# Cross-attention block: one unit kind for all attention units, queries kept in SBUF, one-piece subtractions, another order

## The chip, the core and the metric

The kernel runs on one core of a Trainium2 chip. The metric is the time of one execution on the device in microseconds (us); the runs before the change have a median of 717.12 us (714.55 to 719.68 in 3 runs). The engines are TensorE (PE in the profile, PEld for its weight loads), VectorE (DVE), ScalarE (ACT), GpSimd (POOL) and SyncE (SP), which here issues every DMA.

## The reference

Eight sequences of 256 tokens and 512 channels, with a context of the same shape, go through a transformer block with cross-attention and an MLP, all in float32:

```python
x = layer_norm(hidden_states, ln1_w, ln1_b)
q = (x @ q_w + q_b)                      # 16 heads of 32 channels
k = (encoder_hidden_states @ k_w + k_b)
v = (encoder_hidden_states @ v_w + v_b)
scores = einsum('bhqd,bhkd->bhqk', q, k) / sqrt(32)
scores = where(mask, scores, finfo.min)
attn = softmax(scores, axis=-1)
out = einsum('bhqk,bhkd->bhqd', attn, v) @ cproj_w + cproj_b
hidden = out + hidden_states
y = gelu(layer_norm(hidden, ln2_w, ln2_b) @ fc_w + fc_b)   # 2048 wide, tanh form
return hidden + y @ proj_w + proj_b
```

## The kernel before

**Stages.** The sequences are taken in two groups `g` of four (1,024 tokens). For each group the kernel loads context and tokens, normalizes the tokens, transposes both through TensorE (`turn_*`), and makes keys, values and queries (`keys_of` L946, `values_of` L962), then attention (`attention` L1403), the output projection (`output` L1414), the first MLP product (`fc`) and the second (`proj`). Every dense product is done in blocks by a scheme with seven products in place of eight (at two levels in the MLP): sums and differences of the operand blocks (`sums` L834, `minus` and `plus` L645) are made on VectorE or GpSimd, and results are added up on VectorE as they leave the three PSUM banks X, Y and W (`quad` L855). All TensorE work is float32, but for one bf16 product below.

**Units of attention.** A unit `u` = (g, hg, b) is one group `hg` of four heads (4 x 32 = 128 partitions) of one sequence `b`: 256 queries by 256 keys, four heads at once in tiled matmuls. There are 32 units. `units_of` (L1368) gives their order, and in `attention` the scores of unit n stand beside the value products of unit n − 3 (`LOOK = 3`). Queries, keys and values of each unit are loaded from DRAM (`qu`, `ku`, `vu`, 128 KB each; `operands_of` L977), to which `keys_of` and `values_of` stored them in pieces of 256 KB (`qd`, `kd`, `vd`).

There are two kinds of units. `KINDS` sets which is which: the first eight of group 0 are of kind `a`, the other 24 of kind `p`.

- Kind `p` (`scores` L994, `attend` L1037): one score product `s` with the keys on the partitions; ACT copies it out with the mask's bias (`ev`, 8 copies of 128x256, through `copy` L643); VectorE takes the maxima over the keys, by two transposing reductions over 128x1024 (`mx`, L1007), a transpose (`mt`, L1011), three small ACT copies (`mc`, L1014) and a reduction (`fold`, L1015). The 32x32 maxima are stored to DRAM (`md`) and loaded back as a broadcast to all partitions (`mm`, 128x1024, 512 KB). The maxima are subtracted in two halves `less` (L1027), each of them two instructions of 128x512, on VectorE or GpSimd; ACT takes the exponential in place (128x1024, L1030). `attend` makes sums by a product with ones and the value products in one PSUM bank (`av`), VectorE makes the reciprocals (`r`: L1053, L1055, L1056) and multiplies (`att`).
- Kind `a` (`scores_a` L1060, `attend_a` L1116): a first score product `s` with the queries on the partitions; VectorE negates, adds the mask (`mb`) and reduces in one instruction for each head and 128 queries (`max`, L1076, 8 of 128x256, each with an instruction that reads the accumulator); the maxima are split into two bf16 halves (`hl`, L1090 to L1092), transposed (`t2`), stored (`me`) and loaded as rows (`mr`); ACT takes a first exponential only for its row sums (L1082). The reciprocals (`rs`, `tr`, `rd`) go through DRAM and come back in four broadcast loads (`rl`, 32 KB each). A second product `sT` starts from a bf16 product that puts the negated maxima into PSUM, adds the scores with the keys on the partitions, and ACT takes the exponential straight from there (`pt`, L1128). Then value products `av` and `att`.

**The order.** The kernel's code only records operations. `PROGRAM` (L126) is a written-out list of all 3,076 operations in the order in which they are issued; each engine takes its own in that order, and a letter after an operation's name names its engine where there is a choice (`:V` VectorE, `:A` ACT, `:G` GpSimd). `PLACES` (L369) gives each tile its slot in SBUF or its bank in PSUM; a tile waits until the one before it in its slot is done with. `SLOTS` has the number of slots: 44 places of 128x1024 (kind Q; kind P takes halves of them), 14 of 128x256 for `qu`, `ku`, `vu` and `r`. So nothing is decided at run time, and where a wait ends late, all that stands behind it in that engine's list is late. All DMAs are in SP's list, which is in order too.

In the profile L663 is the matmul helper, L654 the addition helper, L630, L635 and L643 copies out of PSUM, L617 and L623 the issue of a load and of a store.

Of the kernel before, what the change touches and what calls it, by code (L numbers as in the profile page):

```python
# [10 lines left out]
F32 = mybir.dt.float32  # L11
U8 = mybir.dt.uint8
BF16 = mybir.dt.bfloat16
# [6 lines left out]
FLT_MAX = 3.4028234663852886e38  # L20
# [3 lines left out]
SLOTS = {"Q": (44, 1024), "P": (36, 512), "H": (14, 256), "sm": (10, 32), "mx": (3, 352), "st": (6, 32), "MB": (4, 256), "MU": (4, 64), "t2": (3, 32), "MR": (3, 256)}  # L24
# [102 lines left out]
cq0_10_1 cq0_01_1 cq0_01_0 cq0_00_1 cq0_00_0 cq0_10_0 vw00 rows6 cq0_11_1 turn_c0_01 xt0_1 turn_c0_11 rows3 c0_01:V  # L127
cq0_11_0 turn_c0_10 rows5 turn_c0_00 kw10 c0_10:V c0_00:A turn_c0_30 c0_11:V kw00 turn_c0_20 xt0_3 c0_30:V c0t1:G
v0_0_P1 mk xt0_2 stats_x0_01 kw11 c0_20:V vw01 turn_c0_21 v0_0_t1:A v0_1_P1 rows2 c0_21:V xt0_0 aggr_x0_01 xt0_6
kws3:V turn_c0_31 rows7 stats_x0_11 k0_0_P1 rows1 c0_31:A stats_x0_10 rows4 aggr_x0_10 xt0_5 kws1:V aggr_x0_11  # L130
rows0 kws2:V v0_0_P2 kw01 eps_x0_1 pow_x0_1 stats_x0_00 xt0_7 vw10 aggr_x0_00 mk~1 c0t3:V v0_1_P2 qw00 fw1_01_0
nb_x0_1 eps_x0_0 v0_0_c11 norm_x0_11:A vw11 pow_x0_0 cols fw1_00_1 k0_0_P7 norm_x0_10:A nb_x0_0 cols~1 pw0_10_10
norm_x0_01:V norm_x0_00:A qw01 c0t2:V v0_1_t1:A xt0_4 turn_x0_00 k0_0_t1:A fw1_00_0 turn_x0_20 c0t4:V k0_0_P6 mu0
x0_20:A stats_x0_21 fw1_11_1 x0_00:A stats_x0_30 fw1_01_1 turn_x0_30 aggr_x0_21 k0_0_t2:V pw0_00_10 turn_x0_10
x0_30:A v0_1_c11 pw0_01_01 k0_0_P5 fw1_10_1 vws1:V pw0_00_11 kws4:V pw0_10_00 k0_0_P2 stats_x0_20 vws2:G mu2
aggr_x0_20 k0_0_t3:V vd0_0_11 fw1i1_3:G pw0_00_00 v0_0_P6 fw1i1_1:V x0_10:V fw1i1_2:G qw10 stats_x0_31 k0_0_P3
eps_x0_2 aggr_x0_30 k0_0_c22 pow_x0_2 k0_0_c11 fw1i2_1:G kd0_0_22 aggr_x0_31 fw1_10_0 eps_x0_3 nb_x0_2 k0_0_P4
pow_x0_3 norm_x0_21:A vu000 fw1i2_3:G nb_x0_3 norm_x0_30:A pw0_10_11 norm_x0_31:V fw0_00_0 qws3:G fw1_11_0
pw0_01_00 norm_x0_20:V turn_x0_11 k0_0_c12:V turn_x0_31 k0_0_c21 turn_x0_21 v0_0_t2:V turn_x0_01 kd0_0_21 x0_21:A
vws3:V v0_0_P5 pw0_11_10 x0_01:A fw1i1_4:V fw1s3:V x0_31:A fcd1_1_True qw11 v0_0_P7 v0_0_t3:A pw0_11_00 fw1i2_2:V  # L140
x0_11:A fw0_10_0 kd0_0_11 q0_1_P2 v0_0_c22 pb fw0_10_1 fw1s1:V kd0_0_12 q0_1_P1 qws1:V fcd1_5_False fw1s2:V
fw0_00_1 q0_0_P1 q0_1_t1:A qws2:V fcd1_6_False x0t1:V q0_0_P2 q0_0_t1:A x0t2:V mb2:V fw1s4:V q0_0_P6 q0_1_c11
x0t3:V q0_1_P6 qd0_1_11 q0_0_t2:A fcd1_3_False vd0_0_22 x0t4:V fcd1_7_False q0_0_P5 pw0_11_11 q0_0_c11 pw0_10_01
fw1i6_3:V fw0_11_1 fw1i2_4:V v0_0_P4 q0_1_t2:V fw1i4_3:G vd0_1_11 qd0_0_11 fw0s3:V fw0_11_0 q0_1_P7 pw0_11_01
fw1i6_1:V cb fw1i5_1:V fw1i6_2:G qu010 ku002 qws4:V q0_1_P5 fcd1_2_True mb0:G v0_0_c21 fw1i4_1:V fw1i5_2:V qu000
q0_0_P7 fw1i5_3:V fw1i5_4:G fw0s1:V k0_1_P1 q0_0_t3:A fw1i6_4:V q0_1_t3:A q0_0_c22 fcd1_6_True q0_0_P3 qd0_0_22
k0_1_t1:A fw0i1_1:V ku020 fw0s2:V pw0_01_10 ku000 fw0i1_2:G q0_0_P4 fcd1_5_True fw1i4_2:V ku022 q0_1_c22 fw0i5_1:G
fw0i5_2:G q0_1_P4 q0_0_c21 fw0i1_4:G q0_0_c12:V qd0_0_21 qd0_1_22 k0_1_P6 q0_1_c21 pw0_00_01 fw0_01_0 fw0i6_3:V
fw1i4_4:V qd0_0_12 vws4:V s000 qu020 fw0i5_4:V fw0_01_1 fw0i6_1:V fw1i3_1:V v0_0_P3 fcd0_5_False max000_5 fw1i3_2:V
fw0i6_2:V max000_2 fw1i3_4:G max000_4 v0_1_P6 fw1i3_3:G v0_0_c12:V fw0i6_4:V vd0_0_12 max000_7 fcd0_6_True max000_6  # L150
q0_1_P3 max000_3 fcd1_3_True fw0i1_3:V qu022 max000_1 max000_0 qu002 fw0i2_1:V s020 fcd1_4_True hl000 ct1_4 fw0s4:V
exp000_7 k0_1_P7 v0_1_t2:A k0_1_t2:A max020_1 fw0i2_2:V q0_1_c12:A max020_0 fw0i2_4:G max020_5 exp000_0 k0_1_P5
t2000 max020_7 fw0i2_3:G exp000_2 max020_2 exp000_1 max020_4 fcd0_2_True max020_3 qd0_1_21 max020_6 s002 k0_1_t3:A
hl020 me000 exp000_5 fcd0_1_True k0_1_c22 k0_1_P2 exp000_4 t2020 max002_0 exp020_5 me020 max002_1 exp000_3
fcd0_6_False max002_3 exp000_6 vd0_0_21 pw0s1:G v0_1_P5 exp020_0 ct1_3 rs000 max002_7 exp020_6 qd0_1_12 max002_4
exp020_2 qu032 max002_5 tr000 k0_1_P4 max002_2 mr000 v0_1_t3:A max002_6 fw0i5_3:G k0_1_c11 hl002 kd0_1_11 s022
# [206 lines left out]
pr17_P4 z1i4_4:G pr14_P6 pr17_c21 pr17_21~1:V out1_1022:G pr14_P2 out1_1012:V pr13_c21 out1_1112:G pr14_t2  # L363
pr17_22~1:V out1_0122:G pr14_P5 out1_0112:G pr17_12:G pr14_P7 out1_0121:G pr14_t3 st1_111 st1_011 out1_1111:V
out1_0111:V pr17_11:V st1_010 pr14_P3 pr17_12~1:V pr17_21:V pr14_c11 st1_110 pr14_c22 pr14_P4 pr14_c12 st1_101
pr14_c21 st1_100
"""

PLACES = """  # L369
# [1150 lines left out]
```

## Time and profile before

| | |
|---|---|
| median of 3 runs | 717.12 us (714.55 to 719.68) |
| profiled execution | 713.26 us |
| its span, first to last instruction | 711.4 us |
| mean granted TensorE clock | 0.999 |
| first score product, first one of kind `p`, last value product | 70.9, 173.7, 410.8 us |
| instructions in the span | 13,452 |

The profile is one execution. Its page gives the busy time of each engine and the costliest groups of instructions: line, engine, operation, tile written and tile read, shape, count, then busy time and mean time of one, then the idle time of the engine just before them and what ended it. TensorE matmuls of float32 show as two instructions each. The trace can be asked for the busy time in any stretch, for all instructions or for those of one tile or line alone, and for the instructions of one engine in order of time.

### The profile page before, as it was taken

How to read it: one execution, taken by the hardware profiler on the slowest of the kernel's cores; microseconds unless marked ns; L12 is line 12 of the kernel's file. 1: busy time of each engine (PE TensorE's matmuls, PEld its weight loads, DVE VectorE, ACT ScalarE, POOL GpSimd, SP SyncE). 2: the span in 40 equal slices, each digit the busy share in tenths (PEclk: the TensorE clock that was granted, in tenths of full speed). 3: DMA queues.
4: the chain of work that ended last, by engine and by line, in shares of the span. 5: the costliest groups of instructions: out<-in, count | busy, mean ns of one | idle time of the engine just before them, and what ended most of it. 6: DMA issues, size and time to landing. Idle time of an engine off the chain costs nothing. (4 is left out here: it accounts for less than half of the span.)

```text
span 711.4 us, 13452 instructions
## 1 busy us (share of the span) xinstructions
PE 682.7 (96%) x4813; PEld 528.5 (74%) x4813; DVE 602.5 (85%) x1125; ACT 345.3 (49%) x775; POOL 325.9 (46%) x310
## 2 busy tenths in 40 slices
PE   8989989999999998999999999999999999999997
PEld 7554555655544575667766789999998888899997
DVE  5988898859999989999899889796888777898863
ACT  1431479968995748967999846001400005730000
POOL 2403352604754567787686655703353004722134
PEclk9999999999999999999999999999999999999999
DMA  8989988888867898768445545338958632851552
GB/s 282 303 289 327 341 265 273 296 282 270 279 211 221 264 300 267 218 196 270 129 155 177 150 130 174 119 104 266 296 163 262 210 100 49 270 164 60 178 193 89
DMA packets 119321, 152.82 MB, mean 215 GB/s; under 512 B 13164, under 2 KB 80344, under 8 KB 119256
## 3 DMA queue, kind: packets, MB, share of 16 engines
q1 hardware_dynamic: 119256, 151.98, 66.7%
q8 instruction: 38, 0.62, 0.3%
q14 instruction: 27, 0.22, 0.1%
HBM read 107.60 MB, written 44.34 MB: 214 GB/s over the span
## 5 line engine op out<-in xcount | busy, mean ns | idle before, releaser
L1027 POOL TENSOR_TENSOR pr<-pr,mm 128x512 f32<-128x512 f32 x64 | 83.9, 1341 | 61.5 <-DMA mm<-md 29.2
L643 ACT ACTIVATE pr<-s,cols 128x256 f32<-128x256 f32 x192 | 77.7, 481 | 9.7 <-PE s L663 5.9
L1285 ACT ACTIVATE h<-h,cols 128x256 f32<-128x256 f32 x128 | 53.9, 496 | 48.8 <-DVE h L654 45.7
L654 DVE TENSOR_TENSOR h<-fc_X,h 128x512 f32<-128x512 f32 x80 | 53.2, 678 | 10.9 <-PE fc_X L663 8.4
L1007 DVE TRANSPOSE_TENSOR_REDUCE mx<-pr 128x32 f32<-128x1024 f32 x48 | 58.0, 1221 | 4.9 <-ACT pr L643 4.9
L1030 ACT ACTIVATE pr<-pr 128x1024 f32<-128x1024 f32 x48 | 50.4, 1061 | 14.2 <-POOL pr L1027 9.6
L1082 ACT ACTIVATE pr<-pr,st 128x256 f32<-128x256 f32 x64 | 32.0, 516 | 17.4 <-DVE st L1092 16.8
L654 DVE TENSOR_TENSOR h<-fc_W,h 128x512 f32<-128x512 f32 x48 | 32.1, 677 | 7.9 <-PE fc_W L663 7.8
L663 PE MATMUL s<-qu,ku 32*128 32x256 f32 x384 | 28.6, 400 | 3.6 <-ACT pt L1128 1.4
L1128 ACT ACTIVATE pt<-sT,cols 128x256 f32<-128x256 f32 x64 | 25.5, 483 | 8.1 <-PE sT L663 4.1
L663 PEld LDWEIGHTS s<-qu,ku 32*128 32x128 f32 x384 | 18.4, 184 | 14.8 <-ACT pr L643 5.5
L630 ACT COPY e<-pr_X 128x256 f32<-128x256 f32 x3 | 1.1, 372 | 57.9 <-PE pr_X L663 57.9
L663 PE MATMUL av<-pr,ones 128*32 128x256 f32 x384 | 26.0, 385 | 1.5 <-ACT pr L1030 0.8
L1027 DVE TENSOR_TENSOR pr<-pr,mm 128x512 f32<-128x512 f32 x32 | 25.9, 857 | 1.8 <-DMA mm<-md 1.8
L654 POOL TENSOR_TENSOR h<-h,fl 128x512 f32<-128x512 f32 x3 | 4.7, 1595 | 48.1 <-DVE fl L654 48.1
L654 DVE TENSOR_TENSOR po<-pr_X,po 128x256 f32<-128x256 f32 x40 | 16.4, 414 | 11.2 <-PE pr_X L663 10.9
L663 PE MATMUL av<-pr,vu 128*32 128x256 f32 x384 | 25.5, 379 | 0.0
L1076 DVE CUSTOM_DVE_ANT_0 pr<-s,mb 128x256 f32<-128x256 f32 x64 | 23.3, 417 | 1.8 <-PE s L663 1.6
L1014 ACT COPY mx<-mx 32x64 f32<-32x64 f32 x72 | 17.5, 243 | 12.7 <-DVE mx L1011 11.2
L663 PE MATMUL fc_W<-y1i,fl 128*128 128x256 f32 x92 | 23.5, 381 | 0.0
L663 PEld LDWEIGHTS av<-pr,ones 128*32 128x32 f32 x384 | 10.5, 109 | 15.0 <-issue 4.9
L630 ACT COPY h<-fc_X 128x512 f32<-128x512 f32 x11 | 6.2, 582 | 31.6 <-PE fc_X L663 31.6
(568 smaller groups left out, 1974.7 us busy)
## 6 DMA issues: line engine op xcount, KB each, us to landing
mm<-md SPq DMA_DIRECT2D x24, 512.0 KB
fl<-fcd SPq DMA_DIRECT2D x48, 256.0 KB
pl<-prd SPq DMA_DIRECT2D x46, 256.0 KB
fl<-prd SPq DMA_DIRECT2D x21, 256.0 KB
fw<-in_L_xattn_fc_w_dram SPq DMA_DIRECT2D x16, 256.0 KB
pw<-in_L_xattn_proj_w_dram SPq DMA_DIRECT2D x32, 128.0 KB
vu<-vd SPq DMA_DIRECT2D x32, 128.0 KB
qu<-qd SPq DMA_DIRECT2D x32, 128.0 KB
```

Of the source, the lines that this page charges most:

```text
L630: (nc.scalar.copy if e == "ACT" else nc.vector.tensor_copy)(to(), of_())
L643: lambda e: nc.scalar.activation(to(), of_(), AF.Identity, bias=bias(), scale=1.0))
L654: E[e].tensor_tensor(to(), in0(), in1(), op)
L663: nc.tensor.matmul(o(), l(), r(), start=first, stop=True, skip_group_check=True)
L1007: T.op(f"mx{u}_{h}", [("DVE", 1.126)], [(pr[h], None)], [(mx, [h])], lambda e, h=h: nc.vector.tensor_reduce(tile_of(mx)[:, 0:64].rearrange ...
L1014: lambda e, a=a: nc.scalar.copy(tile_of(mx)[0:32, 64 + 64 * a : 128 + 64 * a], tile_of(mx)[32 * a : 32 * a + 32, 64:128]))
L1027: E[e].tensor_tensor(p_, p_, at(M, j)[:, None, :].to_broadcast([P, 2, S]), ALU.subtract)
L1030: lambda e, h=h: nc.scalar.activation(tile_of(pr[h]), tile_of(pr[h]), AF.Exp), table="exp")
L1076: nc.vector.tensor_tensor_reduce(at(p_, pk), at(sb[j], i), tile_of(mb), scale=-1.0, scalar=FLT_MAX, op0=ALU.add, op1=ALU.min, accum_out=ti ...
L1082: nc.scalar.activation(at(p_, pk), at(p_, pk), AF.Exp, bias=tile_of(st)[:, 24 + c : 25 + c], scale=-1.0, accum_out=tile_of(st)[:, 16 + c : ...
L1128: nc.scalar.activation(at(pt[j // 2], 2 * (j % 2) + kc), at(sT[j], kc), AF.Exp, bias=col(2 * (4 * g + b) + kc), scale=1.0)
L1285: lambda e, f=f, b=b, c=c: nc.scalar.activation(at(h[f][b], c), at(h[f][b], c), AF.Gelu_apprx_tanh, bias=col(c_fcb + f * 4 + c), scale=1.0 ...
```

## The change

- `KINDS` is `p` for all 32 units. `scores_a` and `attend_a` go, with the tiles, constants, mask tiles and small DMAs that only they use.
- `DIRECT` names the query pieces that need not pass through DRAM. "K": the unit reads its queries in the tile that the projection wrote, and nothing is stored (all eight pieces of group 1). "H": the same for the first half of the piece's columns; the piece is stored and the second half is loaded as before (all eight of group 0). So 8 of 16 query stores and 8 of 32 query loads are left. Keys and values go as before.
- `less` on VectorE is one instruction of 128x1024 for a half; on GpSimd it stays two of 128x512. Of 64 halves the new order gives 28 to VectorE and 36 to GpSimd; before it was 16 and 32 of 48.
- `PROGRAM` and `PLACES` are new throughout: 2,928 operations, with another order and other slots and, for operations that several engines can do, in part another engine. `SLOTS` has 45 places of kind Q for 44. In the built programs GpSimd has 180 additions or subtractions of 512 elements for 151, and 115 of 256 for 109; VectorE has fewer. DMA issues are 577 for 651.

```diff
-SLOTS = {"Q": (44, 1024), "P": (36, 512), "H": (14, 256), "sm": (10, 32), "mx": (3, 352), "st": (6, 32), "MB": (4, 256), "MU": (4, 64), "t2": (3, 32), "MR": (3, 256)}
+SLOTS = {"Q": (45, 1024), "P": (36, 512), "H": (14, 256), "sm": (10, 32), "mx": (3, 352)}
...
-KINDS = ("aaaaaaaapppppppp", "pppppppppppppppp")
+DIRECT = {
+    "q0_0_11": "H", "q0_0_12": "H", "q0_0_21": "H", "q0_0_22": "H", "q0_1_11": "H", "q0_1_12": "H",
+    "q0_1_21": "H", "q0_1_22": "H", "q1_0_11": "K", "q1_0_12": "K", "q1_0_21": "K", "q1_0_22": "K",
+    "q1_1_11": "K", "q1_1_12": "K", "q1_1_21": "K", "q1_1_22": "K",
+}
+KINDS = ("pppppppppppppppp", "pppppppppppppppp")
...
-            store(dr.name, dr, None, [(b, None)], lambda dr=dr: dr.t, lambda b=b: tile_of(b), 0.26)
+            way = DIRECT.get(b.name, "")
+            if way != "K":
+                store(dr.name, dr, None, [(b, None)], lambda dr=dr: dr.t, lambda b=b: tile_of(b), 0.26)
             for l in range(2):
-                d[g, 2 * I + mc, 2 * Lh + l] = (dr, lambda dr=dr, l=l: dr.t[:, ts(l, 256)])
+                d[g, 2 * I + mc, 2 * Lh + l] = (dr, lambda dr=dr, l=l: dr.t[:, ts(l, 256)]) if way == "" or (way == "H" and l) else (
+                    None, b, lambda b=b, l=l: tile_of(b)[:, ts(l, 256)])
...
             def less(e, h=h):
+                if e == "DVE":
+                    p_ = tile_of(pr[h]).rearrange("p (i k q) -> p i k q", i=2, k=2)
+                    m_ = tile_of(M)[:, 512 * h : 512 * h + 512].rearrange("p (i q) -> p i q", i=2)
+                    nc.vector.tensor_tensor(p_, p_, m_[:, :, None, :].to_broadcast([P, 2, 2, S]), ALU.subtract)
+                    return
                 for i in range(2):
...
-    def scores_a(g, hg, b):
...
-    def attend_a(g, hg, b, u, q, k, v, mr, R):
...
-                made[n] = scores_a(*units[n]) if KINDS[g][n] == "a" else scores(*units[n], KINDS[g][n] == "z")
+                made[n] = scores(*units[n], KINDS[g][n] == "z")
             if n >= LOOK:
-                (attend_a if KINDS[g][n - LOOK] == "a" else attend)(*units[n - LOOK], *made.pop(n - LOOK))
+                attend(*units[n - LOOK], *made.pop(n - LOOK))
```

More of the change, by code (lines that the diff above doesn't have):

```diff
@@ L132 @@
[L132 to L141, printed above, removed]
```

831 lines of the change are left out of this document (365 added, 466 removed).

## The prediction

> **What bounds the kernel now.** I read the page's shares first, then a table of the engines by stage, then the order of TensorE's (PE's) work around single attention units.
>
> ```profile
> span 711.4 us, 13452 instructions
> ...
> PE 682.7 (96%) x4813; PEld 528.5 (74%) x4813; DVE 602.5 (85%) x1125; ACT 345.3 (49%) x775; POOL 325.9 (46%) x310
> ...
> L1027 POOL TENSOR_TENSOR pr<-pr,mm 128x512 f32<-128x512 f32 x64 | 83.9, 1341 | 61.5 <-DMA mm<-md 29.2 <-DMA r<-rd 24.0 <-DVE mx L1015 4.3
> ```
>
> TensorE is busy nearly always, VectorE (DVE) comes next. I cut the span where the first attention unit starts (71 us), where the first of the other kind starts (174), where the second MLP input begins (279) and where the last unit ends (413). Columns: PE, PEld, DVE, ACT, POOL busy, then clock, DMA share, GB/s.
>
> ```profile
> 0.00:71.00 71.00, 65.56 (x245) 39.99 (x245) 56.34 (x100) 17.58 (x25) 20.33 (x43) 1.00 0.91 300
> 71.00:174.00 103.00, 94.76 (x692) 59.21 (x691) 86.02 (x276) 77.30 (x243) 36.72 (x40) 1.00 0.88 290
> 174.00:279.00 105.00, 99.95 (x716) 60.07 (x720) 99.57 (x178) 76.96 (x152) 64.48 (x57) 1.00 0.81 256
> 279.00:413.00 134.00, 130.00 (x1061) 94.09 (x1053) 121.15 (x208) 113.06 (x222) 98.61 (x83) 1.00 0.61 190
> 413.00:711.40 298.40, 292.39 (x2112) 275.13 (x2112) 239.43 (x367) 60.40 (x134) 105.78 (x89) 1.00 0.52 165
> ```
>
> After 413 us PE idles 2%, with VectorE at 80%: pure TensorE time, which the change leaves alone. In 71 to 413 PE is busy 324.7 of 342 us and VectorE 306.7 (90%): two engines nearly full at once. PE idles most (8 of 103 us) in 71 to 174, where the eight units of the kind that is abolished lie, and VectorE is nearest to full (95%) in 174 to 279, where all units are of the kind that stays. DMA is no bound: its share falls from 0.91 to 0.52 while PE fills up. The clock is 1.00 throughout.
>
> **TensorE, old unit against new.** Both kinds as they stand in the order of time (start, length, what):
>
> ```profile
> 133.14 0.59 PE L663 MATMUL v_W<-vw,c1t 128*128 128x256 f32 x2
> 133.88 0.40 PE L663 MATMUL sT<-mr,picks 32*128 32x512 bf16 x4 [0.15 <-DVE st L1076]
> ...
> 135.07 1.07 PE L663 MATMUL av<-pt,vu 128*32 128x256 f32 x16
> 136.07 1.99 PE L663 MATMUL v_W<-vw,c1t 128*128 128x256 f32 x8
> 137.91 1.88 PE L663 MATMUL k_Y<-c,kw 128*128 128x512 f32 x4
> ...
> 140.72 1.15 PE L663 MATMUL s<-qu,ku 32*128 32x256 f32 x16
> 141.79 1.99 PE L663 MATMUL v_X<-qws,c 128*128 128x256 f32 x8
> ```
>
> ```profile
> 307.17 1.15 PE L663 MATMUL s<-qu,ku 32*128 32x256 f32 x16
> 308.25 1.07 PE L663 MATMUL av<-pr,ones 128*32 128x256 f32 x16
> 309.13 1.05 PE L663 MATMUL av<-pr,vu 128*32 128x256 f32 x16
> 310.11 1.13 PE L663 MATMUL fc_X<-y0i,fl 128*128 128x256 f32 x4
> ```
>
> And one row of the chain of waits, four matmuls of 128x256 that follow one another:
>
> ```profile
> 609.99 0.86 PE fc_W L663 x4
> ```
>
> From start to next start an old unit costs 1.07 (s) + 1.19 (sT) + 1.00 (av) = 3.26 us, a new one 1.08 + 1.86 = 2.94: 0.32 us less. It also has two groups in tiled mode for three, and each group costs something at its edges: the eight v_W matmuls behind the av group take 1.84 us, where four of that shape in a row are 0.86, so 0.11 more; ahead of the sT group 133.88 − 133.14 is 0.74 for 0.43 of work, 0.31 more, half of it a wait. I take 0.17 a group. Eight units: 8 × (0.32 + 0.17) = **3.9 us** of TensorE work less; 3.4 to 4.5 by the two edge prices.
>
> **VectorE, old unit against new.** Busy time by tile or line over the whole run, one fence each: the negated maxima of the old kind (L1076, 64 with their accumulators); its bf16 splitting and transpose (tile hl); then two smaller groups of it and the subtraction; then the tile mx of the 24 new units (DVE, then ACT) and their reciprocals (tile rc).
>
> ```profile
> 0.00:711.40 711.40, 23.40 (x128) 1.00 0.67 215
> ```
>
> ```profile
> 0.00:711.40 711.40, 9.24 (x32) 0.42 (x6) 1.00 0.67 215
> ```
>
> ```profile
> L1027 DVE TENSOR_TENSOR pr<-pr,mm 128x512 f32<-128x512 f32 x32 | 25.9, 857 | 1.8 <-DMA mm<-md 1.8
> ...
> L654 DVE TENSOR_TENSOR x1t<-x,x1t 128x1024 f32<-128x1024 f32 x2 | 2.9, 1453 | 0.0
> ...
> L654 DVE TENSOR_TENSOR x0t<-x,x 128x1024 f32<-128x1024 f32 x2 | 2.4, 1216 | 0.0
> ...
> L1107 DVE STREAM_TRANSPOSE tr<-st 128x32 f32<-128x32 f32 x8 | 1.6, 197 | 0.0
> L1105 DVE RECIPROCAL st<-st 128x8 f32<-128x8 f32 x8 | 1.5, 193 | 0.9 <-ACT pr L1082 0.9
> ```
>
> ```profile
> 0.00:711.40 711.40, 77.03 (x96) 17.47 (x72) 1.00 0.67 215
> ```
>
> ```profile
> 0.00:711.40 711.40, 25.77 (x72) 1.00 0.67 215
> ```
>
> Last the subtraction's own line on both engines, with minimum, median and maximum:
>
> ```profile
> L1027 POOL TENSOR_TENSOR pr<-pr,mm x64: 1264/1282/2077, 165.2 to 384.5; 128x512 f32<-128x512 f32 x64
> L1027 DVE TENSOR_TENSOR pr<-pr,mm x32: 647/683/1778, 165.0 to 407.5; 128x512 f32<-128x512 f32 x32
> ```
>
> Old: (23.40 + 9.24 + 1.6 + 1.5) / 8 = 4.47 us a unit. New, without the subtraction: (77.03 + 25.77) / 24 = 4.28. So the swap itself gives VectorE back only 8 × 0.19 = 1.5 us. The new kind then owes subtractions: VectorE now does 16 halves in 25.9 us (1.62 each, two instructions), and after the change 28 halves of one 128x1024 instruction each. No such instruction with a broadcast operand is in the trace; the nearest plain ones took 1216 and 1453 ns, so 34 or 41 us, 8 to 15 more. I take 1.23, near the lower row: the median of a 512-wide piece with the broadcast operand is 683, so two are 1.37 with two starts, and one start less brings that to the lower row, not the upper one. GpSimd (POOL) takes 36 halves for 32: 4 × 2 × 1341 = 10.7 us more.
>
> The slowest VectorE subtraction took 1.10 us over the median, somewhat under one POOL instruction of 1.28, and the mean lies 857 − 683 = 174 ns over it: about 0.17 us of waiting each, 28 × 0.17 = 5 us if the single pieces wait as often.
>
> The Trainium skill, "SBUF — State Buffer", Who interferes with whom, says that a VectorE tensor_tensor with both inputs in SBUF and a GpSimd instruction block each other for the whole instruction. The 1778 agrees with it. By that rule the 28 pieces are an estimate of 39 us in place of 34, and the rule speaks against a change that gives GpSimd more work.
>
> **The order.** The built program moves other work from VectorE to GpSimd: beside the subtractions 21 more 512-wide sums, 6 more 256-wide. To price a whole new order without its trace I gave each instruction of both built orders the mean time that its group holds its engine in this trace, and summed by stage. For 71 to 413 this gives VectorE 307.6 us where the table above shows 306.7, so the sums can be trusted to a per cent. From the first score product to the last value product, before and after: PE 320.7 and 302.9, VectorE 307.6 and 299.2, ACT 252.4 and 240.1, POOL 203.4 and 221.2. The stage loses 17.8 us of TensorE work, of which 3.9 are gone and 13.9 are dense products that the new order does after the last unit.
>
> How long will the stage be? At the same ratio of time to TensorE work, 302.9 × 342 / 320.7 = 323 us. At the same VectorE share, 299.2 / 0.897 = 334. These are the ends. In 174 to 279, the stage with new units alone, VectorE was held at 0.948, and 299.2 / 0.948 = 316 lies under the first end, so the ratio of TensorE decides; but in the new order the largest surplus of VectorE work over TensorE work in any stretch is 12 us (6.5 now), so I add 1: **324, 18 less**. The 13.9 us reappear behind it at that stage's ratio, 298.4 us for 291.6 of work: **14.2 more**.
>
> At the start, the first transposes need the first two context quarters of the SP queue, where they need the second and third now:
>
> ```profile
> 0.72 3.00 SPq L617 DMA_DIRECT2D cq<-in_ctx_dram  x6
> ```
>
> ```profile
> 6.13 5.11 PE L770 MATMUL ps_c<-ident,cq 128*128 128x128 f32 x24 [1.92 <-DMA cq<-in_ctx_dram]
> ```
>
> TensorE waits 1.92 us for them. One issue is 3.00 / 6 = 0.5 us; VectorE's work up to the first unit falls by 3.5 us in the sums. I take **1 us less**, 0 to 2.
>
> **Queries in SBUF** cost no instruction. The page's bytes:
>
> ```profile
> DMA packets 119321, 152.82 MB, mean 215 GB/s; under 512 B 13164, under 2 KB 80344, under 8 KB 119256
> ```
>
> The change of DMAs: 24 of 32 loads (128 KB) and 8 of 16 stores (256 KB) go. Eight more broadcast loads of 512 KB come, and 32 reciprocal loads of 32 KB and their stores go: about 2 MB less of 152.8 in all, and 74 fewer issues on SP. Since DMA bounds nothing, I cost this at nothing; the cover is the early loading of operands, and if slots held longer by queries delay a load, it shows as a TensorE wait on it, bounded by ±2 us. The added pairs of store and load of maxima make SP and POOL wait:
>
> ```profile
> SPq L623 <- DVE mx L1015: 43.6, 16, 6.4
> ```
>
> 16 waits of 2.7 us each for 24 units; eight more units add some 15 to 22 us of SP waiting, behind which operand and MLP weight loads are queued. SP loses as much: 74 issues of 0.5 us. On POOL the wait for the broadcast (29.2 us in the page row above) holds up weight and token sums; POOL goes to 221 of 324 us, 68%, so it has room.
>
> **Sum.** −18 + 14.2 − 1 = −4.8 us: a span of 706.6. The profiled execution took 713.26 us, 1.8 around its span, and 3.9 below the median of the runs, 717.12; I take the difference over: **712 us**.
>
> **Rivals.** A change under 1% (7.2 us) can't be told from none here.
>
> *The stall goes with its cause.* PE's idle share in the attention falls to that of 279 to 413 (0.970 busy for 0.949 over the three stages): 323 × 0.949 / 0.970 = 316, so −26 + 14.2 − 1 = −13, 704 to 706 us. For it: value products stand farther behind their scores in the new order. Against it: VectorE would have to be at 0.947 over all of the stage.
>
> *VectorE becomes the bound (slower).* 299.2 us of VectorE at 0.897 makes the stage 334, −8 + 14.2 = +6; with the 5 us of waits on POOL, over 0.897, +11.5: 723 to 728 us. It decides where the share that VectorE reaches between first score and last value product stays under 299.2 / 328 = 0.91. For it: VectorE's work there falls by 3% only, TensorE's by 6%, and POOL's rises. Against it: the 0.948 already reached.
>
> *Only the arithmetic shows.* New stalls eat all but the 3.9 us, or less: 713 to 717. This is also the case in which the swap does not relieve the 71 to 174 stretch.
>
> **Chances.** Forecast 0.45 (712, own range 707 to 717), relief 0.25, VectorE bound 0.18, arithmetic 0.12. Faster by over 1% (under 709.9): a third of the forecast's range and nearly all of the relief, 0.15 + 0.25 = 0.40. Slower by over 1% (over 724.3): most of the VectorE case, 0.15, and a little for an order that fails elsewhere, 0.17. Within 1%: 0.43. The range reaches from the relief case, 703.5, to the cheaper half of the VectorE case, 722.
>
> **What would show it.** Right: PE busy near 679, no sT group; attention ends near 70 + 324 = 394 us, VectorE over 0.91 busy until there, PE idling about 2% behind it; one-piece subtractions at 1.2 to 1.3 us; POOL busy near 365. Wrong: subtractions at 1.45 and more with POOL waiting in turn; the attention ending after 400 us; PE waiting on qu, ku or vu loads, or for slots; or stalls of PE in the last 300 us, which I took over unchanged.

## The result, and the profile after

| | before | changed |
|---|---|---|
| median (range) on the same chip | 717.63 us (714.55 to 719.68) | 697.74 us (695.50 to 700.01) |
| profiled execution | 713.26 us | 700.01 us |
| its span | 711.4 us | 698.2 us |
| head: to the start of the first score product | 70.9 us | 68.5 us |
| attention: from there to the start of the last value matmul | 341.5 us | 318.9 us |
| tail: from there to the end | 299.0 us | 310.7 us |

The ratio is 0.9726 (95% interval 0.9676 to 0.9776). Two more measurements of the changed kernel on other chips, below, gave 0.980 and 0.979, so the gain is 2 to 2.7 per cent, 13 to 20 us. The forecast was 712 us, the range 703.5 to 722: the direction was right, the gain was 2.6 to 3.9 times the forecast one, and the time lies outside the range.

From the page of the changed kernel: busy time of each engine, then the two groups that subtract the maxima (L994 and L999 were L1027), then the bytes.

```profile
span 698.2 us, 13106 instructions
...
PE 677.9 (97%) x4781; PEld 527.6 (76%) x4781; DVE 592.3 (85%) x970; ACT 339.5 (49%) x695; POOL 376.3 (54%) x328
...
DMA packets 112183, 150.44 MB, mean 215 GB/s; under 512 B 10188, under 2 KB 73208, under 8 KB 112120
...
L999 POOL TENSOR_TENSOR pr<-pr,mm 128x512 f32<-128x512 f32 x72 | 97.7, 1386 | 28.7 <-DMA mm<-md 19.8
...
L994 DVE TENSOR_TENSOR pr<-pr,mm 128x1024 f32<-128x1024 f32 x28 | 36.4, 1318 | 0.0
```

TensorE has 4.8 us less work (682.7 before). The other 8.4 us of the 13.2 that the span lost was time in which TensorE had stood still.

The changed kernel by stage, cut at the first score product, at 154 us (nine of the 32 units have had their score product), at the second MLP input and at the last value product. Columns: PE, PEld, DVE, ACT, POOL busy, then clock, DMA share, GB/s.

```profile
0.00:68.50 68.50, 63.55 (x253) 40.23 (x253) 50.13 (x96) 20.55 (x31) 20.22 (x25) 1.00 0.94 323
68.50:154.00 85.50, 80.92 (x505) 43.52 (x508) 79.71 (x131) 55.79 (x124) 39.45 (x43) 0.98 0.87 293
154.00:288.00 134.00, 127.72 (x1089) 81.42 (x1082) 128.69 (x225) 118.18 (x251) 105.15 (x86) 1.00 0.79 246
288.00:388.00 100.00, 99.88 (x766) 75.03 (x763) 91.04 (x147) 81.50 (x149) 80.50 (x69) 1.00 0.61 192
388.00:698.20 310.20, 305.83 (x2180) 287.39 (x2176) 242.75 (x375) 63.52 (x142) 131.01 (x109) 1.00 0.52 165
```

Read it against the table before the change. From 288 to 388 TensorE stands still for 0.1 us in 100, where the last stage of the attention before had 4 in 134. From 68.5 to 154 and from 154 to 288 VectorE is 93 and 96 per cent busy: what TensorE still loses in the attention, it loses there. The clock of 0.98 from 68.5 to 154 is new too, and the experiments come back to it. Behind the attention TensorE idles 1.4 per cent, 2.0 before.

The attention alone, one row for each kernel, with the same columns: before, then changed.

```profile
70.91:412.37 341.46, 324.16 (x2450) 213.15 (x2452) 306.82 (x659) 267.33 (x616) 199.18 (x178) 1.00 0.75 241
```

```profile
68.55:387.47 318.92, 307.94 (x2346) 199.84 (x2349) 298.87 (x501) 255.03 (x522) 224.52 (x196) 0.99 0.76 242
```

TensorE's share went from 0.949 to 0.966, VectorE's from 0.899 to 0.937, GpSimd's from 0.58 to 0.70. The 22.5 us that the stage lost are 16.2 of TensorE work (most of it dense products that now stand behind the last unit) and 6.3 of idle time.

### The profile page after: what moved, and what is told of

It is laid out like the page before. It is cut to its first block, busy times and chain, and to the rows that moved or that the text cites. A ratio compares the mean times of both kernels' runs of the same rounds, so it can differ in the third digit from the quotient of the medians.

```text
span 698.2 us, 13106 instructions
## 1 busy us (share of the span) xinstructions
PE 677.9 (97%) x4781; PEld 527.6 (76%) x4781; DVE 592.3 (85%) x970; ACT 339.5 (49%) x695; POOL 376.3 (54%) x328
## 4 chain that ended last, share of the span: by engine, by line
PE 61%; DVE 10%; ACT 5%; DMA 2%; issue 2%; SPq 1%; ACTq 0%; DVEq 0%
PE fc_X L641 14%; PE pr_X L641 14%; PE fc_W L641 7%; PE pr_W L641 7%; PE av L641 4%; PE pr_Y L641 4%; PE fc_Y L641 4%; DVE mx L974 3%; PE o_X L641 3%; ACT pr L621 2%; PE s L641 1%; ACT pr L1002 1%; PE ps_y L726 1%; DMA kd<-xt 1%; DVE pr L994 1%
## 5 line engine op out<-in xcount | busy, mean ns | idle before, releaser
L621 ACT ACTIVATE pr<-s,cols 128x256 f32<-128x256 f32 x256 | 104.5, 483 | 25.4 <-PE s L641 22.7
L999 POOL TENSOR_TENSOR pr<-pr,mm 128x512 f32<-128x512 f32 x72 | 97.7, 1386 | 28.7 <-DMA mm<-md 19.8
L974 DVE TRANSPOSE_TENSOR_REDUCE mx<-pr 128x32 f32<-128x1024 f32 x64 | 76.5, 1217 | 0.3 <-ACT pr L621 0.3
L1002 ACT ACTIVATE pr<-pr 128x1024 f32<-128x1024 f32 x64 | 66.8, 1068 | 7.8 <-DVE pr L994 7.2
L632 DVE TENSOR_TENSOR h<-fc_X,h 128x512 f32<-128x512 f32 x80 | 53.6, 681 | 13.3 <-PE fc_X L641 12.2
L994 DVE TENSOR_TENSOR pr<-pr,mm 128x1024 f32<-128x1024 f32 x28 | 36.4, 1318 | 0.0
L981 ACT COPY mx<-mx 32x64 f32<-32x64 f32 x96 | 23.1, 243 | 16.2 <-DVE mx L978 12.7
L632 POOL TENSOR_TENSOR h<-h,fl 128x512 f32<-128x512 f32 x14 | 18.5, 1337 | 14.4 <-DVE fl L632 13.9
L641 PEld LDWEIGHTS av<-pr,vu 128*32 128x32 f32 x512 | 17.4, 110 | 10.6
L641 PE MATMUL fc_X<-y1i,fl 128*128 128x256 f32 x96 | 24.5, 379 | 0.0
L641 PE MATMUL fc_X<-y0i,fl 128*128 128x256 f32 x88 | 22.5, 382 | 0.0
L641 PE MATMUL s<-q,ku 32*128 32x256 f32 x240 | 20.2, 419 | 1.1 <-DVE att L632 0.9
L982 DVE TENSOR_REDUCE mx<-mx 32x32 f32<-32x256 f32 x32 | 18.4, 578 | 2.5 <-ACT mx L981 2.4
```

The lines of the kernel that those rows point to most:

```text
L621: lambda e: nc.scalar.activation(to(), of_(), AF.Identity, bias=bias(), scale=1.0))
L632: E[e].tensor_tensor(to(), in0(), in1(), op)
L641: nc.tensor.matmul(o(), l(), r(), start=first, stop=True, skip_group_check=True)
L974: T.op(f"mx{u}_{h}", [("DVE", 1.126)], [(pr[h], None)], [(mx, [h])], lambda e, h=h: nc.vector.tensor_reduce(tile_of(mx)[:, 0:64].rearrange ...
L981: lambda e, a=a: nc.scalar.copy(tile_of(mx)[0:32, 64 + 64 * a : 128 + 64 * a], tile_of(mx)[32 * a : 32 * a + 32, 64:128]))
L982: T.op(f"fold{u}", [("DVE", 0.38)], [(mx, [2, 3, 4, 5])], [(mx, [6])], lambda e: nc.vector.tensor_reduce(tile_of(mx)[0:32, 320:352], tile_ ...
```

## The experiments

Each median is compared with runs of the kernel before on the same chip; the ratio to them is given with its 95% interval.

### Two parts undone in the new order

**VectorE's subtractions in two instructions.**

```diff
             def less(e, h=h):
-                if e == "DVE":
...
-                    nc.vector.tensor_tensor(p_, p_, m_[:, :, None, :].to_broadcast([P, 2, 2, S]), ALU.subtract)
-                    return
                 for i in range(2):
```

> The changed kernel, with the 28 subtractions on VectorE cut into two instructions again; order and places as changed. VectorE's subtractions go from 36.4 us (1.30 a half) to about 28 x 1.62 = 45 us. If VectorE sets the length of the attention stage in the new order (it is busy 94% of it), the kernel loses most of these 9 us: 704 to 707 us against 697.7. If TensorE's list sets it and VectorE only follows closely, 0 to 3 us: 698 to 701.

703.31 us, 0.9813 (0.9766 to 0.9859): between the two expectations. Its attention, then its group of subtractions:

```profile
68.49:392.11 323.62, 310.10 (x2345) 200.54 (x2348) 309.15 (x529) 255.80 (x522) 222.53 (x196) 0.99 0.75 239
```

```profile
L994 DVE TENSOR_TENSOR pr<-pr,mm 128x512 f32<-128x512 f32 x56 | 44.9, 850 | 0.0
```

VectorE has 10.3 us more work in the attention, and the attention is 4.7 us longer. So VectorE's time is neither free nor the whole bound. How much of it arrives at the end is uncertain: the attention of two more profiles of the changed kernel, below, is 4.0 and 7.6 us shorter than this one, and by the ratios (0.9813 against 0.9726, 0.980 and 0.9787) the time is 0.1 to 0.9 per cent longer, 1 to 6 us.

**The query traffic, issued for nothing.** The 8 stores and 24 loads that the change saved are issued again, into slots that nobody reads; the units still read the projection's tile.

```diff
-            if way != "K":
-                store(dr.name, dr, None, [(b, None)], lambda dr=dr: dr.t, lambda b=b: tile_of(b), 0.26)
+            store(dr.name, dr, None, [(b, None)], lambda dr=dr: dr.t, lambda b=b: tile_of(b), 0.26)
...
             if d[g, hg, b][0] is None:
                 out.append(d[g, hg, b][1:])
+                buf = Buf(f"{n}u{u}", "H")
+                load(buf.name, buf, None, lambda buf=buf: tile_of(buf), lambda dr=dr, b=b: dr.t[:, ts(b % 2, 256)], 0.13, src=[(dr, None)], lead=1.0)
                 continue
```

> The changed kernel, with the 8 query stores and 24 query loads that it saves issued all the same, into places that nothing reads: 32 issues on SP, 5 MB. The units still read their queries where the projection left them. If the saved traffic and issues carry part of the gain: 701 us or more. If only the shortened way from projection to score product counts, or neither: 697 to 699.

705.08 us, 0.9844 (0.9798 to 0.9891). The traffic costs, although the mean DMA share of the attention is 0.80 with it (0.76 without). The stretch from the first output projection to the second MLP input (as a row of the engines), and what TensorE waited for in it (total, times, longest):

```profile
229.87:291.45 61.58, 56.61 (x501) 37.84 (x500) 56.63 (x109) 49.87 (x106) 52.69 (x38) 1.00 0.86 274
```

```profile
PE o_X L635 <- DVE a0t L626: 2.3, 1, 2.3
PE s L635 <- DMA ku<-kd: 1.3, 1, 1.3
PE av L635 <- ACT pr L615: 1.2, 1, 1.2
```

The changed kernel passes the same stretch with the same TensorE work 2.9 us faster, at a DMA share of 0.76, and there TensorE waits for no transfer:

```profile
229.66:288.30 58.64, 56.55 (x501) 38.14 (x499) 57.22 (x109) 49.65 (x106) 51.27 (x38) 1.00 0.76 238
```

```profile
PE av L641 <- ACT pr L621: 1.2, 1, 1.2
PE o_X L641 <- DVE hid L632: 0.7, 1, 0.7
```

Two more profiles without the traffic, both below (the second one of the changed kernel and the one with small DMAs), take 59.4 and 58.8 us for this stretch, and one with it (both parts undone) 61.1. The longest wait, 2.3 us, can be followed back, here in the order of GpSimd's and VectorE's work:

```profile
240.12 3.50 POOL L997 TENSOR_TENSOR pr<-pr,mm 128x512 f32<-128x512 f32 x2 [2.58 <-DMA mm<-md]
248.49 2.22 DVE L626 TENSOR_TENSOR a0t<-att,a0t 128x1024 f32<-128x1024 f32 x1 [1.75 <-POOL hid L1321]
```

GpSimd waits 2.58 us for a broadcast of maxima (0.31 to 0.86 us at this place in the three profiles without the traffic, 2.90 in the other with it). Its list is in order, so its sum `hid` comes late, VectorE's sum `a0t` waits for that, and TensorE for `a0t`.

**Issues or bytes?** The same 32 DMAs at the same places in SP's list, but each of one partition. It was run on the same chip as the changed kernel once more and the kernel with both parts undone at once.

```diff
+                store(dr.name, dr, None, [(b, None)], lambda dr=dr: dr.t[0:1, :], lambda b=b: tile_of(b)[0:1, :], 0.26)
...
+                load(buf.name, buf, None, lambda buf=buf: tile_of(buf)[0:1, :], lambda dr=dr, b=b: dr.t[0:1, ts(b % 2, 256)], 0.13, src=[(dr, None)], lead=1.0)
```

> The changed kernel once more, on the chip of the other runs of this call, as their baseline. Expected: 696 to 700 us, ratio 0.970 to 0.978 to the kernel before, attention (first score product to last value product) 317 to 321 us. If its attention differs by more than 2 us between the two profiles, differences of 3 us between single profiles (the 2.9 us of the dead query traffic) prove nothing.

> The changed kernel with the 8 query stores and 24 query loads issued again at the places of the run with dead query traffic, but each moves only one partition (2 KB or 1 KB in place of 256 KB or 128 KB). Theory A: what the saved queries bring is SP's time (32 issues of about 0.5 us, behind which operand and weight loads are queued): then this kernel is as slow as the one with the full traffic, 4 us or more over the changed kernel of this call. Theory B: it is the bytes, 4 to 5 MB that share the DMA engines with the operand, broadcast and weight loads: then it is within 1.5 us of the changed kernel. Rival: neither, the difference of the full traffic was a shift of single DMAs: then anything between.

> The changed kernel with both parts undone: VectorE's subtractions in two instructions, and the full dead query traffic. It keeps the new units and the new order. If the two losses add (VectorE's time and DMA's are paid in different places): 4.7 + 2.9 = 7.6 us over the changed kernel in the profile, attention about 326 us, time 706 to 710. If both only fill the same slack: no more than the larger of the two, attention 323 to 324, time 703 to 705. The forecast of 324 us for the attention counted neither part as a gain; 326 here would say that the missing 5 us of the forecast are these two parts.

The changed kernel: 699.84 us, 0.980 (0.9777 to 0.9822), a little over the ratio expected. The small DMAs: 700.14, 0.9807 (0.9782 to 0.9833), 0.3 us over it. So the 32 issues cost nothing that can be told (the difference is uncertain by some 2.4 us), and theory A, 4 us or more, is out: what the full traffic costs comes from what it moves, its bytes and packets. Both parts undone: 708.54, 0.9924 (0.9898 to 0.995), **8.7 us** over the changed kernel. That is the time expected if the two losses add (706 to 710). The attention isn't: its 322.7 us lie under both expectations, 326 and 323 to 324:

```profile
70.92:393.60 322.68, 308.92 (x2345) 200.62 (x2348) 305.43 (x529) 255.37 (x522) 224.01 (x196) 0.99 0.80 255
```

Between this profile and that of the changed kernel on the same chip (spans 704.0 and 695.4) 6.7 us lie in the attention and 2.1 in the head. The profile with both parts undone is one of its faster executions (705.8 us); the 8.7 us rest on medians of 7 and 5 executions and are uncertain by some 2.5.

Single profiles tell less than that: the two of the changed kernel differ by 2.9 us in the attention (318.9 and 316.0). Nearly all of it lies at one spot, here in the first profile, then in the second:

```profile
90.11 0.44 PE L726 MATMUL ps_c<-ident,qws 128*128 128x128 f32 x1 [1.56 <-DMA qws<-in_ctx_dram]
90.48 2.09 PE L641 MATMUL s<-q,ku 32*128 32x256 f32 x16
92.50 2.52 PE L641 MATMUL v_X<-vws,c 128*128 128x256 f32 x8
```

```profile
89.49 1.15 PE L641 MATMUL s<-q,ku 32*128 32x256 f32 x16 [0.32 <-ACT c L608]
90.57 1.99 PE L641 MATMUL v_X<-vws,c 128*128 128x256 f32 x8
```

In the first TensorE waits 1.56 us for a piece of the context, and the two groups behind it take 1.47 us more. The granted clock is 0.50 there from 90.5 to 93.5 us; in the second profile it is 1.00 throughout. Such stretches of some 3.4 us at half clock, each worth about 1.7 us, stand in some executions and not in others: one in the attention of the first and the third profile of the changed kernel and of the one with subtractions in two instructions, two in the one with both parts undone, none in the kernel before and none in the attention with the full traffic. A wait alone does not bring them: with the full traffic TensorE waits 1.87 us at the same spot, and the clock stays at 1.00. What does is not shown. Over all executions the mean clock is 0.996 for the changed kernel on this chip and 0.993 with both parts undone, so up to 2 us of the 8.7 can come by the clock.

> The kernel before, unchanged, for a second profile. If the first profile (713.26 us; attention 341.5, head 70.9, tail 299.1) was a fast execution of its kind, this one comes out at 714 to 718 with the difference spread over the stages; if the difference sits in one stage, that stage is where executions of this kernel differ, and a comparison of single profiles there is worth no more than that.

714.66 us; head 71.6, attention 342.6, tail 298.7. The first profile of the kernel before was an ordinary one, its stages within 1.1 us of this.

### The same parts in the old order

**One piece in the kernel before**: the five lines of `less` put into it.

> The kernel before, with the 16 subtractions on VectorE as one instruction each and nothing else changed. 16 x 0.32 = 5 us of VectorE work less, between 165 and 408 us. If the one-piece subtraction carries the gain: 712 to 713 us. If the order and the kinds of units carry it: 716 to 718, no difference that can be measured.

712.95 us, 0.9955 (0.992 to 0.999): 3.2 us by the ratio (0.7 to 5.7), 1.6 by the medians. The profile, a slower execution (714.7 us), shows an unchanged attention (341.3), so where the gain arises is not shown.

**Queries direct, alone and with one piece.** The changed kernel's code for queries in the kernel before; its tiles live longer, and 204 tiles had to get another slot. Beside them stands the changed kernel with the rest of the query traffic taken off (146 tiles in other slots):

```diff
-    "q0_0_11": "H", "q0_0_12": "H", "q0_0_21": "H", "q0_0_22": "H", "q0_1_11": "H", "q0_1_12": "H",
+    "q0_0_11": "K", "q0_0_12": "K", "q0_0_21": "K", "q0_0_22": "K", "q0_1_11": "K", "q0_1_12": "K",
```

> The kernel before, in its own order and with both kinds of units, but with the changed kernel's handling of queries: 8 of 16 query stores and 24 of 32 query loads are left out, and the units read the projection's tile. 204 tiles got another slot for it. Theory A: the bytes taken off the DMA engines are worth about 6 us wherever the attention shares them with operand and broadcast loads: 705 to 710 us here, the gain in the attention. Theory B: they are worth something only in the new order, whose operands are loaded shortly before use: 711 to 715. Rival: the tiles held longer make loads wait for slots, over 716.

> The same with VectorE's subtractions in one instruction too: both parts without the new units and the new order. If the parts carry their gain by themselves: about 3 us under the run with the queries alone, 702 to 708 us, which would leave 5 us or less of the gain to units and order. If they need the new order: 709 to 714.

> The changed kernel with the rest of the query traffic gone too: all pieces of group 0 are read in the projection's tile as a whole, so 8 more stores of 256 KB and the last 8 query loads of 128 KB go, 3 MB. 46 places of kind Q for 45 and 10 of 128x256 for 14; 146 tiles have another slot; the order is the same. If bytes decide, 3 MB less bring about half of what 5 MB more cost, 2 to 3 us under the changed kernel: 695.5 to 698, ratio 0.970 to 0.976 (the changed kernel has 0.973 to 0.980). If bytes matter only past a certain load that the changed kernel is already under: 698 to 700. If the fewer slots make loads wait: over 701.

737.77 us, 1.0319 (1.0286 to 1.0352); 736.9, 1.0295 (1.0265 to 1.0325); 712.2, 0.9959 (0.9941 to 0.9976). The first two are 21 to 22 us slower than the kernel before, the third 11 to 17 slower than the changed kernel by the ratios. For the first and the third only the rivals had allowed for that, for the second nothing. Either longer-lived query tiles cost that, or the other slots do. So the next three kernels leave the slots alone and take traffic away by other means: units that lose their load read the queries of one early unit. A fourth moves slots and nothing else.

```diff
-            store(dr.name, dr, None, [(b, None)], lambda dr=dr: dr.t, lambda b=b: tile_of(b), 0.26)
+            if name != "q" or g == 0:
+                store(dr.name, dr, None, [(b, None)], lambda dr=dr: dr.t, lambda b=b: tile_of(b), 0.26)
...
+        if g == 1 or b % 2 == 0:
...
+            q = first_q[0]
```

> The kernel before, its order, its units and all its slots as they are, without 8 of the 16 query stores and 23 of the 32 query loads (4.9 MB); the units that lose their load read the first unit's queries (so it computes other scores in 23 units). No tile has another slot. Theory A: the bytes are worth 3 to 6 us in any order: ratio to the kernel before 0.991 to 0.996. Theory B: they are worth something only in the new order: 0.998 to 1.002.

> The same with VectorE's subtractions in one instruction. One piece alone gave 0.9955 in the old order. If both parts carry their gain by themselves: 0.987 to 0.992. If the query part needs the new order: 0.994 to 0.998; then most of the gain of the change stays with the new order that makes the parts pay.

> The changed kernel with its slots and order as they are, without 7 of the 8 query stores and 7 of the 8 query loads that it still has (2.7 MB); those 7 units read the queries of the first such unit (other scores in 7 units). If bytes still decide: 2 to 3 us under the changed kernel, ratio 0.970 to 0.975. If the changed kernel is already under the load from which bytes matter: 0.975 to 0.980.

> The changed kernel, all operations and their order as they are, but 134 tiles of kinds Q and P in other slots, found by the same procedure as in the runs with the queries direct in the old order, with the rest of the query traffic gone, and with all units of the new kind in the old order. If the losses of those runs (14 to 22 us where they re-placed 146 and 204 tiles) come from the slots: 706 us or more, attention 327 us or more. If they come from the queries' tiles living longer: 697 to 702, and slots are no part of it.

- Traffic alone in the old order: 712.51 us, 0.9975 (0.9947 to 1.0003). Between the expectations: a gain of 0 to 4 us.
- Both parts in the old order: 709.9 us, 0.9928 (0.9903 to 0.9952), some 5 us, again between the expectations.
- The changed kernel without the rest of its traffic: 697.97 us, 0.9766 (0.9737 to 0.9794), within the second expectation; no further gain can be told.
- Other slots alone: 714.07 us, 0.9971 (0.9946 to 0.9997). **Re-placing 134 tiles, with every operation and the order the same, gives back nearly the whole gain**, as the first expectation has it (attention 329.4 us). Two rows show a part of it, from the order of VectorE's work, then of TensorE's:

```profile
88.61 0.75 DVE L606 TENSOR_SCALAR q<-q_X,cols 128x512 f32<-128x512 f32 x1 [5.21 <-DMA fcd<-fw0i]
```

```profile
89.41 3.78 PE L632 MATMUL q_X<-x,xt 128*128 128x512 f32 x4 [4.21 <-DVE q L606]
```

A piece of queries had got the slot of a weight sum that SP's store to DRAM was still reading. VectorE, which should copy the piece out of PSUM, waited 5.21 us for that store, and TensorE 4.21 us for the PSUM bank. The four matmuls behind that took 3.78 us, where the same four take 1.88 us otherwise: the clock stood at 0.50, in all for some 10 us of this attention, 8 of them with TensorE busy (some 4 us lost). The mean clock of all executions is 0.992, that of the run without the rest of the traffic 0.998, which makes some 4 us of the 16 between the two.

So the three runs with new slots say nothing about queries.

### The units alone

All 32 units of the new kind in the old order: each old operation replaced, word for word, by those of the new kind that stand for it, two instructions for each subtraction on VectorE. 144 tiles have another slot here too.

> The kernel before with all units of kind p: each operation of the eight old units is replaced in its place in the old order (maxima by copies, split and transposes by the maxima's reduction, the second score product by the subtractions, its exponentials by the in-place ones); 144 tiles get other slots, and the subtractions stay in two pieces. If the kind of units carries the gain by relieving the stretch from 71 to 174 us, 705 to 710 us. If the order carries it, TensorE's 3.9 us at best: 713 to 718.

765.21 us, 1.0672 (1.0617 to 1.0728): both expectations fell. The longest of its waits in question:

```profile
POOL pr L994 <- DMA mm<-md: 56.8, 14, 12.8
...
ACT mx L981 <- DVE mx L978: 40.9, 14, 7.5
...
ACT pr L997 <- DVE pr L994: 23.6, 10, 6.7
```

Each link of the chain from scores over maxima and their broadcast to the exponentials waits (GpSimd's wait for the broadcast was 29.2 us before, with 24 such units). But slots alone cost 14 us above, so these 50 us can't be put down to units in the old order. What the units bring without the new order stays open.

### VectorE relieved without another change

Six of VectorE's 28 halves go to GpSimd, nothing else (`less022_1`, `less030_1`, `less001_0`, `less021_0`, `less023_1`, `less011_0`: `:V` becomes `:G`).

> The changed kernel with six of VectorE's 28 subtraction halves, one in each of six units of group 0 (between about 115 and 235 us, where VectorE is 92 to 99 per cent busy and GpSimd 47 to 72), given to GpSimd; order and slots as they are. VectorE has 6 x 1.22 = 7.3 us less there, GpSimd 6 x 2 x 1.3 = 16 us more, and a half takes 1.4 us longer. If VectorE's time sets the attention (two instructions for one added about 11 us to it and 3 to 5 us to the span): 2 to 4 us under the changed kernel of this call. If the longer half on GpSimd takes back what VectorE gets: within 1.5 us. If GpSimd's list, which stands in order behind the broadcast loads, is the tighter one: over 2 us slower.

> The changed kernel again as the baseline of this call: 696 to 700 us, ratio 0.973 to 0.980.

699.94 us, 0.9789 (0.9766 to 0.9813), and the changed kernel 699.66, 0.9787 (0.9755 to 0.9819): no difference, as the second expectation has it. The groups and the attention, first of the baseline, then of the run with six halves moved:

```profile
L999 POOL TENSOR_TENSOR pr<-pr,mm 128x512 f32<-128x512 f32 x72 | 97.8, 1389 | 27.1 <-DMA mm<-md 20.9
...
L994 DVE TENSOR_TENSOR pr<-pr,mm 128x1024 f32<-128x1024 f32 x28 | 34.6, 1256 | 0.6 <-DMA mm<-md 0.6
```

```profile
68.52:388.12 319.60, 308.24 (x2345) 199.99 (x2348) 297.29 (x500) 254.94 (x522) 225.01 (x196) 0.99 0.76 242
```

```profile
L999 POOL TENSOR_TENSOR pr<-pr,mm 128x512 f32<-128x512 f32 x84 | 121.3, 1474 | 17.9 <-DMA mm<-md 14.8
...
L994 DVE TENSOR_TENSOR pr<-pr,mm 128x1024 f32<-128x1024 f32 x22 | 31.4, 1436 | 0.0
```

```profile
69.91:391.72 321.81, 310.04 (x2345) 200.85 (x2348) 298.15 (x495) 255.19 (x522) 246.11 (x208) 0.99 0.74 240
```

VectorE got nothing back in these profiles: the attention has 298.15 us of its work after six instructions of 1.2 us left, and 297.29 before (297.7 and 298.9 in the two other profiles of the changed kernel). A subtraction on VectorE takes 180 ns more on average, which makes 4.0 us for the 22, and one on GpSimd 85 ns; the rest is spread over other groups. The profile of this run is the slowest of its six executions (703.78 us). So this run did not lower the load that it meant to lower, and it can't say what a freer VectorE would bring.

## Why the prediction was off

In spans the forecast was 706.6 us and the profile shows 698.2, 8.4 less: 4.5 in the attention (22.5 us shorter for the 18 forecast), 2.5 in the tail, 1.4 in the head. The rest of the 14 us between 712 and 697.74 is in the step from profile to median: I carried over the 3.9 us by which the profiled execution of the kernel before lay under its median, and the profiled one of the changed kernel lies 2.3 us over its own. One profile against one profile gives 13.3 us, the medians 19.9, and the two later measurements, with more executions, 13.4 and 16.1. So a good part of the 14 us is the luck of the first few executions or of their chip: by the later ratios the time would be 702 to 703 us, 9 to 10 under the forecast and just outside the range.

**Right.** TensorE's work: 677.9 us busy against "near 679" (in the attention it fell by 16.2 us, not the 17.8 of the sums). The one-piece subtraction: 1.318 us on average, and 1.242 and 1.256 in two other profiles, for the 1.2 to 1.3 said:

```profile
L999 POOL TENSOR_TENSOR pr<-pr,mm x72: 1259/1277/2565, 93.6 to 377.7; 128x512 f32<-128x512 f32 x72
...
L994 DVE TENSOR_TENSOR pr<-pr,mm x28: 1171/1210/2032, 99.2 to 375.1; 128x1024 f32<-128x1024 f32 x28
```

VectorE's work in the attention was summed to 299.2 us and is 298.87. One instruction in place of two saves 0.16 us, as the step argued (medians 1210 ns and twice 683). Of the estimate from the Trainium skill ("SBUF — State Buffer", Who interferes with whom), 39 us in place of 34 for the 28 pieces, the trace shows 36.4, and 34.2 and 34.6 in two other profiles: the waiting is smaller than 0.17 us each, 0.03 to 0.11 us by means and medians. The maxima, 2032 and 2565 ns, lie 822 and 1288 ns over the medians, about two thirds of a GpSimd instruction and one VectorE instruction. The experiment that moved six halves agrees with the rule too: with more work on GpSimd the medians on VectorE hardly move (1212 and 1218 ns), while the means on both engines grow, as single long waits would make them.

**A reading of the kernel before to set right.** The first score product of kind `p` starts at 140.7 us, not at 173.7 (the row at 140.72 in the prediction's first list is one), and the last value product of kind `a` at 175.1. So the stretch from 71 to 174 us holds three units of the new kind besides the eight old ones, and its 8 us of idle time are not those of the old kind alone.

**Step that failed: "so the ratio of TensorE decides".** The forecast kept the share of TensorE's idle time of the old attention and shortened the stage only in proportion to TensorE's work: 324 us. That counts any relief of VectorE and of the DMA engines at nothing. The runs put a size on both: with both undone in the new order the kernel takes 708.54 us, 4.7 less than the kernel before on the same chip, and its profiled attention 322.7 us, where the forecast had 4.8 and 324. What the forecast missed is as large as what those two parts bring in the new order, **8.7 us**. That 4.7 meets 4.8 so closely is partly luck, given the uncertainty of 2.5 us; and the new order and its slots were laid out with both parts in it, so undoing them may cost more than they bring by themselves.
- The one-piece subtraction was priced as work on VectorE only, not for what it spares: two instructions for each of the same 28 halves would have been 10.3 us more of VectorE's time in the attention, and 4.7 us of that reaches the end in one pair of profiles (1 to 6 us by the ratios). In the old order, with 16 halves, it is 3.2 us, uncertain by 2.5.
- "Since DMA bounds nothing, I cost this at nothing", with ±2 us, failed. A mean share of 0.75 says that the engines are not full, not that a transfer lands in time. And the mean hides nearly full stretches: in the changed kernel the share from 68 to 90 us is 0.95. With 5 MB more in the attention a load of keys lands 1.3 us too late for its scores, and a broadcast 2.6 us too late for GpSimd, which holds up the output projection by 2.3. The ratio with the full traffic, 0.9844, is 0.4 to 1.2 per cent over the three of the changed kernel. The saved issues on SP, which the prediction named as the other half, are worth nothing that can be told (0.3 us).

In the old order both parts together bring some 5 us, in the new order 8.7; the difference is little over the uncertainty of both.

**The tail.** 13.9 us of dense products were moved behind the last unit and I charged them at that stage's ratio, 14.2; the stage grew by 11.7. In the kernel before, TensorE waited there for four things, first of all weight loads; in the changed one the list of its waits in this stretch is empty. Before:

```profile
PE pr_X L663 <- DMA pl<-prd: 1.2, 2, 1.0
PE fc_W L663 <- DVE h L654: 0.6, 1, 0.6
```

"The last 300 us, which I took over unchanged" was named as a weak point, and it moved to the good side.

**The head.** 2.4 us gained for 1 said, and 2.7 in a second pair of profiles; the heads of the eight other profiles with the new order and its slots lie between 68.5 and 70.9 us, so a single pair says little. The wait for the context quarters did go (the first transposes start at 4.16 us, after 6.13 before), and a wait for a weight load came, 1.77 us:

```profile
4.16 1.41 PE L726 MATMUL ps_c<-ident,cq 128*128 128x128 f32 x8
7.34 1.97 PE L641 MATMUL v_X<-vw,c 128*128 128x256 f32 x8 [1.77 <-DMA vw<-in_L_xattn_v_w_dram]
```

**The rivals.** "The stall goes with its cause" had the numbers: 316 us of attention at a TensorE share of 0.970. Three profiles show 318.9, 316.0 and 319.6, at 0.966, 0.970 and 0.964; its time, 704 to 706 us, was still too long. Its reason, value products farther behind their scores, is not shown: worked out from the starts in the trace, that distance fell from 41.0 to 39.1 us for the first eight units and rose from 34.4 to 37.9 for the others, and part of the relief goes when the two parts are undone (0.957). What was held against it, that VectorE would have to reach 0.947 over the whole stage, was too strict: 0.937 was enough. "VectorE becomes the bound" decided at 0.91, and that was passed; "only the arithmetic shows" fell with it. The chance of 0.25 for the rival that came nearest was too low, because its condition was worked out from a single share of VectorE and not from what each of the parts spares.

**Open.** How the remaining 4.7 us divide between the new units and the new order, how much of the order is the order of operations and how much the slots, and what sets the stretches at half clock.

## What to carry to other kernels

Where two engines are over nine tenths busy at once, price an edit by what it spares on each of them and don't let the fuller one's ratio set the stage: here 10 us of VectorE's time were worth 1 to 6 us, and 5 MB were worth 3 to 8 us at a mean DMA share of three quarters. The slots of a hand-laid kernel are part of its schedule: an experiment that re-places tiles needs a run that re-places tiles and does nothing else. And compare medians with medians and profiles with profiles; the 4 us carried over from one to the other lay within the spread of the executions.

## What the runs showed of the hardware that was not expected

- 32 DMA issues of one partition added to SP's list cost 0.3 us in all, the same 32 with 128 partitions 3 to 8 us by the ratios. The length of the list is not what counts here, what it moves is.
- A slot whose last reader was a store to DRAM stayed taken until that transfer was through: one VectorE copy waited 5.21 us for it, and TensorE 4.21 behind that.
- Single executions have stretches of some 3.4 us at a granted clock of 0.50 in the middle of dense TensorE work. Two groups of matmuls took 2.09 and 2.52 us in one, and 1.15 and 1.99 us at full clock; this and a wait of 1.56 us make up nearly all of the 2.9 us between two profiles of one kernel.
- Moving six subtractions from VectorE to GpSimd, 7.3 us of work, left VectorE's busy time in the attention where it was (297.29 and 298.15 us): the 22 subtractions that stayed took 4.0 us more in all.
